# Two graph layers: layer 0's softmax sums by VectorE instead of TensorE, its mask by ScalarE, and the last range check in two parts

## The chip, the core and the metric

The kernel runs on one core of one Trainium2 chip. The metric is the device time of one launch in microseconds (us), the median of several runs. PE is TensorE, PEld its weight loads, DVE is VectorE, ACT ScalarE, POOL GpSimd and SP SyncE.

## What is computed

x is 64 x 256 x 512 and adj 64 x 256 x 256, all float32. adj holds zeros and ones, is symmetric and has ones on its diagonal. Two layers follow one another:

```python
# layer 0
feat_proj = feats @ fc_w.T + fc_b
logits = q + k.T                                  # q, k: one number for each token
masked = logits + (1.0 - adj_mat) * -1e9
masked = where(masked >= 0, masked, 0.01 * masked)
x = softmax(masked, axis=-1) @ feat_proj + feats
# layer 1, 8 heads of 64
scores = Q @ K.T / 8 + (a[:, :, None] + c[:, None, :] + b_g + log(adjacency + 1e-9))
out = softmax(scores, axis=-1) @ V + x
```

## The kernel before

The 64 graphs are worked in 32 groups of two graphs (512 tokens, four blocks of 128). Three groups are in work at once. In `step(d, a, f, n, check)` group `f` goes through layer 0 and the projections of layer 1, group `a` (one before) through layer 1's attention, group `d` (two before) gets its last results divided, completed and stored, and for `n` (one ahead) the inputs are loaded and layer 0's weights made. The order on every engine is written out by hand: strings such as `A("both:0 factor:1:0 pv.sum_10")` name the pieces, and each engine takes its instructions in the order in which the pieces are issued.

**Layer 0's weights.** For group `n`, `adjt` (L538) has DVE turn the adjacency in blocks of 32 into `am` and make `e0 = (am - 1) * 1e9` from it, 128 x 1024. `add_eps` (L548) has ACT add 1e-9 to `am` for layer 1. `weights:0` and `weights:1` (L573) have DVE add q and k to `e0` and apply the leak, and ACT take the exponential. In `e0` the neighbours lie along the partitions and in two tiles `jc`, the tokens in the free dimension. A token's sum is over partitions and both tiles.

**Layer 0's sums.** In the next step, when the group is `f`, `sums` (L586) takes eight matmuls of `e0` with a column of ones in 32 of the array's columns, and ACT copies the result, `sms` (L600). They stand behind `totals_1` of group `d` (L875), which adds up its layer 1 sums with four records of matmuls in 64 columns, and share its PSUM bank. `recip` (L602) turns `sms` by a PE transpose and DVE takes the reciprocal. `mix:0` to `mix:3` (L609) are the products `y` of the unnormalised `e0` with x. `ysum:0` to `ysum:3` (L348) are DVE sums of blocks of y, and `pf` is a product in seven parts, scaled by the reciprocal.

**Attention.** `scores:u` (L789) makes two halves of scores, each in a PSUM pair; there are two such pairs (`psc`, bufs=2). ACT takes the exponential of each half (L815), DVE multiplies it by `am` (`factor`, L821), and `both` (L826) adds the halves.

**The first group** is not mixed with others: `features_first` (L634) writes its order out, with the mask, the weights, the differences of weight blocks on DVE (L333 to L336), the sums, the column constants (L248, L315) and the reciprocal.

**The end.** `finish:gr` (L957) turns, divides and completes the last group's results in two halves `hg` and stores them (`store`, L975; the last ones from SP and ACT). `in_range` (L983) tests that all reciprocals lie between 1e-20 and 1e25; it runs after every fourth group as `check`, and at the end in `check_ranges` (L1026), with a PE transpose and a flag. Every engine loads the flag (L1299) and branches on it (L1301): if a value was out of range, a general version would run.

Of the kernel before, what the change touches and what calls it, by code (L numbers as in the profile page):

```python
# [10 lines left out]
F32 = mybir.dt.float32  # L11
I32 = mybir.dt.int32
AF = mybir.ActivationFunctionType
# [12 lines left out]
def kernel(  # L26
# [97 lines left out]
    nc.gpsimd.memset(eps, 1e-9)  # L124

# [36 lines left out]
    def fast():  # L162
        main = ExitStack()
        with main:
# [349 lines left out]
            class Group:  # L514
# [23 lines left out]
                def adjt(self):  # L538

                    g = self.g  # L540
                    self.am = two.tile([P, TPG, GP, N], F32, tag="am", name=f"am_{g}")
                    self.e0 = one.tile([P, TPG, GP, N], F32, tag="e0", name=f"e0_{g}")
                    flat = "p j g i -> p (j g i)"
                    am, e0 = self.am.rearrange(flat), self.e0.rearrange(flat)
                    nc.vector.transpose(am, self.a.rearrange("p j b c -> p (j b c)"))
                    nc.vector.tensor_scalar(e0, am, 1.0, 1e9, ALU.subtract, ALU.mult)
# [39 lines left out]
                def sums(self):  # L586

                    sm = sm0.pop("bank", None)
                    begun = sm is not None
                    sm = (sm if begun else bank(f"sm0_{self.g}"))[:, 0:P]  # L590
                    for jc in range(TPG):
                        for t in range(T):
                            gr, ic = divmod(t, TPG)
                            nc.tensor.matmul(  # L594
                                sm[ts(t, RS), :], lhsT=ones[:, 0, :], rhs=self.e0[:, jc, gr, ts(ic, P)],
                                start=(jc == 0 and not begun), stop=(jc == TPG - 1),
                                tile_position=(0, t * RS), skip_group_check=True,
                            )
                    self.sms = one.tile([P, P], F32, tag="sms", name=f"sms_{self.g}")
                    nc.scalar.copy(self.sms, sm)  # L600

                def recip(self):  # L602
                    pt = bank(f"rc_{self.g}")[:, 0:P]
                    nc.tensor.transpose(pt, self.sms, ident)
                    nc.vector.reciprocal(
                        recip0[:, self.g, :], pt.rearrange("p (t r) -> p t r", t=T)[:, :, 0]
                    )
# [26 lines left out]
                def features_first(self):  # L634
# [31 lines left out]
                    self.adjt()  # L666
                    product(1)
# [8 lines left out]
                    self.sums()  # L676
# [198 lines left out]
                def totals_1(self):  # L875

                    sm0["bank"] = bank(f"tot_{self.g}_1")
                    self.totals(1, sm0["bank"][:, P : P + NC * N // B])
# [78 lines left out]
                def finish(self, gr):  # L957


                    g, nb = self.g, N // B  # L960
                    self.osb[gr] = two.tile([P, NC * N], F32, tag="osb", name=f"osb_{g}_{gr}")
                    for hg in range(2):
                        o = self.osb[gr][:, ts(hg, 512)]
                        blocks = o.rearrange("p (m c) -> p m c", c=B)
                        nc.vector.transpose(o, self.oTs[gr][:, hg, :])
                        nc.vector.tensor_tensor(
                            blocks, blocks,
                            self.rs[:, ts(hg, 2)].rearrange("p n b -> p (n b)").unsqueeze(2).to_broadcast(
                                [P, 2 * nb, B]
                            ), ALU.mult,  # L970
                        )
                        nc.vector.tensor_tensor(o, o, self.xb[gr][:, ts(hg, 512)], ALU.add)
                    self.store(gr, 2 * (nc.sync, nc.scalar) if gr else 4 * (nc.sync,))
# [9 lines left out]
            def in_range(lo, hi, name):  # L983

                n0, n1 = (hi - lo) * T, (hi - lo) * GP * NC * N // B
                ok = one.tile([P, n0 + n1], F32, tag="junk", name=f"ok_{name}")
                for src, a, b in ((recip0[:, lo:hi].rearrange("p g t -> p (g t)"), 0, n0),
                                  (recip1[:, lo % NR : lo % NR + hi - lo].rearrange(
                                      "p g a h b -> p (g a h b)"), n0, n0 + n1)):
                    nc.vector.tensor_scalar(ok[:, a:b], src, R_LOW, None, ALU.is_ge)  # L990
                    nc.vector.scalar_tensor_tensor(
                        ok[:, a:b], src, R_HIGH, ok[:, a:b], ALU.is_le, ALU.mult
                    )
                okp = const.tile([P, 1], F32, tag=f"okp_{name}", name=f"okp_{name}")
                nc.vector.tensor_reduce(okp, ok, AX.X, ALU.min)
                if "all" in checked:
                    nc.vector.tensor_tensor(okp, okp, checked["all"], ALU.min)
                checked["all"] = okp

            def attention_and_layer_0(D, A, F, X, check):  # L1000
# [3 lines left out]
                F("sums")  # L1004
                A("scores:1 pv.p3 pv.p4 factor:0:0 factor:0:1")
                D("ratios:1")
                A("both:0 factor:1:0 pv.sum_10 factor:1:1 both:1")
# [18 lines left out]
            def check_ranges():  # L1026

                in_range(NG - NR // 2, NG, "last")
                pk = bank("pok")
                nc.tensor.transpose(pk[0:1, 0:P], checked["all"], ident)  # L1030

                def flag_ready():
                    oks = one.tile([1, 2], F32, tag="oks", name="oks")
                    nc.vector.tensor_reduce(oks[:, 0:1], pk[0:1, 0:P], AX.X, ALU.min)
                    nc.vector.tensor_copy(flag, oks[:, 0:1])

                return flag_ready

            checked, sm0 = {}, {}

            def step(d, a, f, n, check):
# [41 lines left out]
                if n is None:  # L1083
                    if a is not None:
                        a.totals(1, bank("tot_last")[:, 0 : NC * N // B])
                    A("ratios:1 divide:1 complete:1 store:1")
                    F("residual:1 turn_residual:1")

                    F("pv.p2 scores:0 pv.p6 pv.sum_00 factor:0:0 factor:0:1 scores:1 both:0 pv.p7")
                    F("factor:1:0 factor:1:1 both:1 scores:2 pv.p5 sums_1:0 scores:3 pv.sum_11")  # L1090
                    F("ratios_t:0 ratios_r:0 factor:2:0 factor:2:1 pv.p3 pv.p4 factor:3:0 pv.sum_10")
                    F("factor:3:1 attend:0 finish:0 sums_of_e:1 attend:1")
                    F("ratios_t:1 ratios_r:1 finish:1")
                    check_ranges()()
                    return
                X("add_eps")
# [6 lines left out]
            with tc.manual_schedule(engines=ENGINES):  # L1103
# [10 lines left out]
                for g in range(NG):  # L1114
                    n = Group(g + 1) if g + 1 < NG else None

                    def check():

                        if d is not None and (d.g % NR == NR - 1 or d.g == NG - NR // 2 - 1):
                            in_range(d.g // NR * NR, d.g + 1, f"{d.g}")  # L1120
# [218 lines left out]
```

## Time and profile before

| | us |
|---|---|
| median of 3 runs (lowest, highest) | 2345.28 (2344.49, 2346.56) |
| the profiled execution | 2344.13 |
| its span in the profile | 2342.3 |
| DVE's mask, L546, 32 times | 22.2 in all, 0.694 each |
| PE's old sums, L594, 512 records | 20.6 in all |
| PE's old transpose before the reciprocal, L604, 32 times | 8.7 in all, 0.272 each |

The profile is of one execution. Times in it are from the start of the span. A PE product of 128x256 in float32 shows as two records of matmul, and lengths of records overlap; what PE spends is read from start to start. A line of the timeline has the start, the length, the engine, the source line, the operation, what is written from what, and how many instructions are put together; in brackets is the idle time of the engine before it and who ended it.

### The profile page before, as it was taken

The numbers are of one execution on the slowest core, as the hardware profiler recorded it, in microseconds if no ns is written. First come the engines' busy times: TensorE is split into PE (matmuls) and PEld (weight loads), VectorE is DVE, ScalarE is ACT, GpSimd is POOL, SyncE is SP. The second block draws the span as 40 slices with busy tenths as digits, with TensorE's granted clock in tenths as the row PEclk, the third lists the DMA queues.
The fourth block names the chain that finished last, engine by engine and source line by source line (L and its number), as shares of the span: only waits on it lengthen the run. The fifth ranks groups of instructions, "written<-read, shape, count | busy, mean of one in ns | idle before, by whom it ended". The sixth has DMA issues, their size and how long they took to land.

```text
span 2342.3 us, 34561 instructions
## 1 busy us (share of the span) xinstructions
PE 2324.0 (99%) x13203; PEld 1907.7 (81%) x13203; DVE 2083.5 (89%) x3026; ACT 980.7 (42%) x1710; POOL 130.4 (6%) x111
## 2 busy tenths in 40 slices
PE   9999999999999999999999999999999999999997
PEld 5888888888888888888888888888888888888885
DVE  6798989889889989999899889998998989999897
ACT  3444344444444344444434444434444344444443
POOL 0000000000000000000000000000000000000000
PEclk9999999999999999999999999999999999999999
DMA  4122332223322233322233232332223332223312
GB/s 131 46 59 73 77 82 59 63 64 86 77 73 55 59 81 77 77 61 59 71 78 81 61 64 61 86 77 72 58 61 77 78 79 62 56 71 81 77 50 38
DMA packets 517267, 163.90 MB, mean 70 GB/s; under 512 B 415188, under 2 KB 478696, under 8 KB 517096
## 3 DMA queue, kind: packets, MB, share of 16 engines
q1 hardware_dynamic: 505512, 156.25, 28.9%
q10 hardware_dynamic: 11584, 5.38, 0.8%
q8 instruction: 107, 1.75, 0.3%
q14 instruction: 64, 0.52, 0.1%
HBM read 95.43 MB, written 66.12 MB: 69 GB/s over the span
## 4 chain that ended last, share of the span: by engine, by line
PE 97%; DVE 2%; DMA 1%; issue 0%; ACTq 0%; ACT 0%; DVEq 0%
PE pv L408 17%; PE pq L408 16%; PE pk L408 16%; PE pf L408 16%; PE sc L801 11%; PE y L626 9%; PE oT L841 9%; PE tot L594 1%; DMA x1T<-xd 1%; PE fp L655 1%; PE tot L868 0%; DMA xd<-xt 0%; DVE t1b L373 0%; DMA fc_nat<-in_L_gnn_fc_w_dram 0%; DVE xt L729 0%
## 5 line engine op out<-in xcount | busy, mean ns | idle before, releaser
L821 DVE TENSOR_TENSOR e<-e,am 128x1024 f32<-128x1024 f32 x254 | 303.3, 1215 | 49.7 <-ACT e L815 49.6
L815 ACT ACTIVATE e<-sc,c 128x1024 f32<-128x1024 f32 x254 | 269.2, 1111 | 42.1 <-PE sc L801 42.1
L801 PE MATMUL sc<-qT,kT 64*128 64x256 f32 x2048 | 255.7, 389 | 0.0
L488 POOL TENSOR_TENSOR pf_s<-pf_s,x 128x512 f32<-128x512 f32 x93 | 128.1, 1378 | 2130.4 <-ACT pf_s L487 2022.5
L841 PE MATMUL oT<-e,v 128*64 128x256 f32 x2032 | 233.4, 382 | 0.0
L801 PEld LDWEIGHTS sc<-qT,kT 64*128 64x128 f32 x2048 | 187.2, 186 | 46.5 <-issue 27.5
L626 PE MATMUL y<-e,x 128*128 128x256 f32 x992 | 222.6, 379 | 0.0
L841 PEld LDWEIGHTS oT<-e,v 128*64 128x64 f32 x2032 | 140.1, 137 | 85.5 <-issue 21.3
L626 PEld LDWEIGHTS y<-e,x 128*128 128x128 f32 x992 | 186.1, 190 | 26.3
L425 ACT ACTIVATE pq_s<-pq,cols 128x256 f32<-128x256 f32 x192 | 80.7, 472 | 255.3 <-PE pq L408 255.3
L487 ACT ACTIVATE pf_s<-pf,recip 128x256 f32<-128x256 f32 x186 | 78.1, 471 | 199.3 <-PE pf L408 198.1
L858 DVE TENSOR_REDUCE part<-est 128x32 f32<-128x1024 f32 x124 | 151.3, 1220 | 4.3
L857 DVE STREAM_TRANSPOSE est<-es 128x1024 f32<-128x1024 f32 x124 | 152.4, 1229 | 0.0
L848 ACT COPY oTs<-oT 128x512 f32<-128x512 f32 x128 | 75.1, 587 | 182.6 <-PE oT L841 161.7
L828 DVE TENSOR_TENSOR es<-e,e 128x1024 f32<-128x1024 f32 x126 | 148.4, 1197 | 1.2
L632 ACT COPY yT<-y 128x512 f32<-128x512 f32 x124 | 72.1, 581 | 152.4 <-PE y L626 152.4
L422 ACT COPY pk_s<-pk 128x512 f32<-128x512 f32 x96 | 56.3, 586 | 186.3 <-PE pk L408 186.3
L422 ACT COPY pv_s<-pv 128x512 f32<-128x512 f32 x96 | 55.6, 579 | 185.4 <-PE pv L408 185.4
L408 PE MATMUL pk<-x1T,wk 128*128 128x256 f32 x512 | 124.2, 385 | 0.0
L408 PE MATMUL pq<-x1T,wq 128*128 128x256 f32 x512 | 121.2, 379 | 0.2 <-DMA x1T<-xd 0.2
L408 PE MATMUL pv<-wv,t1b_c 128*128 128x256 f32 x512 | 121.1, 379 | 0.0
L408 PE MATMUL pv<-wv,t1b 128*128 128x256 f32 x512 | 121.1, 379 | 0.0
(176 smaller groups left out, 4466.9 us busy)
## 6 DMA issues: line engine op xcount, KB each, us to landing
x<-in_x_dram SPq DMA_DIRECT2D x32, 1024.0 KB, 5.2
out_dram<-osb SPq DMA_DIRECT2D x254, 128.0 KB, 3.3
xd<-xt SPq DMA_DIRECT2D x124, 256.0 KB, 2.1
x1T<-xd SPq DMA_DIRECT2D x434, 64.0 KB, 2.0
adj<-in_adj_dram SPq DMA_DIRECT2D x128, 128.0 KB, 3.8
qrow<-q SPq DMA_DIRECT2D x31, 256.0 KB, 4.1
x1T<-xd ACTq DMA_DIRECT2D x62, 64.0 KB, 2.5
fc_nat<-in_L_gnn_fc_w_dram ACTq DMA_DIRECT2D x4, 256.0 KB, 3.9
```

Of the source, the lines that this page charges most:

```text
L408: nc.tensor.matmul(o, lhsT=lk[:, ts(m, P)] if len(lk.shape) == 2 else lk[:, m], rhs=rk, start=(start and m == 0 and k == 0), stop=(m == 1 ...
L422: nc.scalar.copy(dst, src)
L425: nc.scalar.activation(dst[:, m], src[:, m], AF.Identity, bias=self.bias[:, 2 * o + m : 2 * o + m + 1],)
L488: nc.gpsimd.tensor_tensor(s, s, self.out(o, k), ALU.add)
L626: nc.tensor.matmul(y[:, ts(gr, N)], lhsT=self.x[:, gr * TPG + j, ts(c, P)], rhs=self.e0[:, j, gr, :], start=(gr == 0 and j == 0), stop=(gr ...
L801: nc.tensor.matmul(sc[:, par, pr, :], lhsT=self.kT[rows, 2 * hg + pr, ts(t, P)], rhs=self.qT[rows, 2 * hg + pr, ts(gr, N)], start=True, st ...
L815: nc.scalar.activation(e, sc, AF.Exp, bias=self.c[:, t : t + 1], scale=SCALE)
L821: nc.vector.tensor_tensor(ef, ef, self.am[:, jc, u // 2, :].unsqueeze(1).to_broadcast([P, 4, N]), ALU.mult,)
L828: nc.vector.tensor_tensor(self.esum[u], self.e[u, 0], self.e[u, 1], ALU.add)
L841: nc.tensor.matmul(oT[par * HD : (par + 1) * HD, pr, :], lhsT=self.v[:, gr * TPG + jc, ts(h, HD)], rhs=self.e[2 * gr + hg, jc][:, par, pr, :],
L857: nc.vector.transpose(turned, self.esum[u].rearrange("p a b i -> p (a b i)"))
L858: nc.vector.tensor_reduce(self.part[:, hg, :], turned.rearrange("p (m c) -> p m c", c=B), AX.X, ALU.add,)
```

## The change

Layer 0's sums: DVE adds the two tiles of `e0` (`add_tiles`), turns the result in blocks of 32 and sums over 32 (`parts_0`), which leaves four partial sums a token, spread over the four bands of 32 partitions. `recip` adds these with four matmuls of a matrix `every` (which has ones where the places in a band agree), each in 32 columns, and DVE takes the reciprocal from PSUM. The matmuls of `sums`, their copy by ACT and the transpose in `recip` go; `totals_1` has a bank to itself. `add_tiles` stands where `sums` stood, `parts_0` after `ratios:1`, and `factor:1:0` now comes before `both:0`.

The mask: two ACT instructions, just before `add_eps` (in the first group just after `adjt`), in place of one on DVE.

The end: the check of all but the last graph's ratios runs between the halves of `finish:0`, that of the last graph's before `finish:1:0`, the flag is set between `finish:1:0` and `finish:1:1`, and the stores follow as before. For this `finish(gr)` becomes `finish(gr, hg)`, the body of its former loop, with the stores issued apart, and `in_range` takes a list of parts, with the same instructions for each part.

```diff
+    minus = const.tile([P, 1], F32, tag="minus", name="minus")
+    nc.gpsimd.memset(minus, -1.0)
...
-                    am, e0 = self.am.rearrange(flat), self.e0.rearrange(flat)
-                    nc.vector.transpose(am, self.a.rearrange("p j b c -> p (j b c)"))
-                    nc.vector.tensor_scalar(e0, am, 1.0, 1e9, ALU.subtract, ALU.mult)
+                    am = self.am.rearrange(flat)
+                    nc.vector.transpose(am, self.a.rearrange("p j b c -> p (j b c)"))
+
+                def mask(self):
+                    flat = "p j g i -> p (j g i)"
+                    am, e0 = self.am.rearrange(flat), self.e0.rearrange(flat)
+                    nc.scalar.activation(e0, am, AF.Identity, bias=minus)
+                    nc.scalar.mul(e0, e0, 1e9)
...
-                def sums(self):
...
+                def add_tiles(self):
+                    self.es0 = two.tile([P, TOK], F32, tag="xt", name=f"es0_{self.g}")
+                    e0, es0 = self.e0, self.es0.rearrange("p (g i) -> p g i", g=GP)
+                    nc.vector.tensor_tensor(es0, e0[:, 0], e0[:, 1], ALU.add)
+
+                def parts_0(self):
+                    turned = two.tile([P, TOK], F32, tag="xt", name=f"es0t_{self.g}")
+                    self.part0 = one.tile([P, TOK // B], F32, tag="part0", name=f"part0_{self.g}")
+                    nc.vector.transpose(turned, self.es0)
+                    nc.vector.tensor_reduce(
+                        self.part0, turned.rearrange("p (m c) -> p m c", c=B), AX.X, ALU.add
+                    )
 
                 def recip(self):
-                    pt = bank(f"rc_{self.g}")[:, 0:P]
-                    nc.tensor.transpose(pt, self.sms, ident)
-                    nc.vector.reciprocal(
-                        recip0[:, self.g, :], pt.rearrange("p (t r) -> p t r", t=T)[:, :, 0]
-                    )
+                    pt = bank(f"rc_{self.g}")[:, 0:T]
+                    for q in range(P // B):
+                        nc.tensor.matmul(
+                            pt[ts(q, B), :], lhsT=every[:, 0:B],
+                            rhs=self.part0.rearrange("p (t q) -> p q t", q=P // B)[:, q],
+                            start=True, stop=True, tile_position=(0, q * B),
+                        )
+                    nc.vector.reciprocal(recip0[:, self.g, :], pt)
...
                     self.adjt()
+                    self.mask()
...
-                    self.sums()
+                    self.add_tiles()
+                    self.parts_0()
...
                 def totals_1(self):
-                    sm0["bank"] = bank(f"tot_{self.g}_1")
-                    self.totals(1, sm0["bank"][:, P : P + NC * N // B])
+                    self.totals(1, bank(f"tot_{self.g}_1")[:, 0 : NC * N // B])
...
             def attention_and_layer_0(D, A, F, X, check):
...
                 D("totals_1")
-                F("sums")
+                F("add_tiles")
                 A("scores:1 pv.p3 pv.p4 factor:0:0 factor:0:1")
                 D("ratios:1")
-                A("both:0 factor:1:0 pv.sum_10 factor:1:1 both:1")
+                F("parts_0")
+                A("factor:1:0 both:0 pv.sum_10 factor:1:1 both:1")
                 check()
                 F("mix:0 mix:1 ysum:0 recip")
...
+            def check_last(part):
+                if part == 0:
+                    r0, r1 = of_groups(NG - NR // 2, NG)
+                    in_range((r0, r1[:, 0 : r1.shape[1] - NC * N // B]), "last")
+                    return
+                in_range((recip1[:, NR - 1, 1].rearrange("p m b -> p (m b)"),), "graph")
+                pk = bank("pok")
+                nc.tensor.transpose(pk[0:1, 0:P], checked["all"], ident)
+                checked["row"] = pk
+
+            def set_flag():
+                oks = one.tile([1, 2], F32, tag="oks", name="oks")
+                nc.vector.tensor_reduce(oks[:, 0:1], checked["row"][0:1, 0:P], AX.X, ALU.min)
+                nc.vector.tensor_copy(flag, oks[:, 0:1])
...
-                    F("factor:3:1 attend:0 finish:0 sums_of_e:1 attend:1")
-                    F("ratios_t:1 ratios_r:1 finish:1")
-                    check_ranges()()
+                    F("factor:3:1 attend:0 finish:0:0")
+                    check_last(0)
+                    F("finish:0:1 store:0 sums_of_e:1 attend:1 ratios_t:1 ratios_r:1")
+                    check_last(1)
+                    F("finish:1:0")
+                    set_flag()
+                    F("finish:1:1 store_last")
                     return
-                X("add_eps")
+                X("mask add_eps")
                 F("pv.p2 pv.p6")
                 X("weights:0")
```

## The prediction

> **What bounds the kernel now.** I read the page first (busy times, then the chain that ended last), then the groups kept apart by form, then the timeline of one group in mid-run, of the first 45 us and of the end.
>
> ```profile
> PE 2324.0 (99%) x13203; PEld 1907.7 (81%) x13203; DVE 2083.5 (89%) x3026; ACT 980.7 (42%) x1710; POOL 130.4 (6%) x111
> PE 97%; DVE 2%; DMA 1%; issue 0%; ACTq 0%; ACT 0%; DVEq 0%
> ```
>
> TensorE (PE) is the bound: 97% of the chain. VectorE (DVE) is 89% busy but is on the chain only at the two ends. So in the 30 middle groups a change counts by what it does to PE's stream, and DVE work counts only where it doesn't fit into DVE's waits. At both ends DVE time counts in full.
>
> ```profile
> 1155.16 2.00 PE L801 MATMUL sc<-qT,kT 64*128 64x256 f32 x16
> 1156.34 2.12 ACT L815 ACTIVATE e<-sc,c 128x1024 f32<-128x1024 f32 x2
> 1157.09 0.31 PE L868 MATMUL tot<-part,every 128*64 128x32 f32 x4
> 1157.33 0.65 PE L594 MATMUL tot<-e,ones 128*32 128x128 f32 x16
> 1157.49 2.36 DVE L821 TENSOR_TENSOR e<-e,am 128x1024 f32<-128x1024 f32 x2 [0.86 <-ACT e L815]
> 1157.90 2.00 PE L801 MATMUL sc<-qT,kT 64*128 64x256 f32 x16
> 1159.83 1.99 PE L408 MATMUL pv<-v_s,t1b_c 128*128 128x256 f32 x8
> 1163.59 0.69 DVE L436 TENSOR_TENSOR v<-pv,pv_s 128x512 f32<-128x512 f32 x1 [1.26 <-PE pv L408]
> 1166.84 0.27 PE L604 MATMUL rc<-ident,sms 128*128 128x128 f32 x1
> 1166.95 3.62 PE L626 MATMUL y<-e,x 128*128 128x256 f32 x16
> 1167.66 0.69 DVE L348 TENSOR_TENSOR tb<-yT 128x512 f32<-128x512 f32 x1 [0.99 <-ACT yT L632]
> ```
>
> In these timeline lines (start, length, what) the old sums occupy PE from 1157.33 to 1157.90, 0.57 us from start to start, and the old transpose before the reciprocal from 1166.84 to 1166.95, 0.11 us. DVE waits 0.86, 1.26 and 0.99 us in the same stretch.
>
> ```profile
> 2298.26 1.89 PE L408 MATMUL pk<-t1b,wk 128*128 128x256 f32 x8
> 2300.08 0.31 PE L868 MATMUL tot_last<-part,every 128*64 128x32 f32 x4
> 2300.31 1.99 PE L408 MATMUL pv<-wv,t1b_c 128*128 128x256 f32 x8
> 2302.24 2.00 PE L801 MATMUL sc<-qT,kT 64*128 64x256 f32 x16
> ```
>
> This is the price of putting a small block of another tile shape between 128x128 products. The chain has 40 such products in 8.63 us, 0.216 each, so 8 take 1.73. Here the 8 before the block take 1.82 (+0.09), the block 0.23, and the 8 after it 1.93, of which I give half of the +0.20 to the switch in and half to the switch out to the scores: 0.09 + 0.23 + 0.10 = 0.42 us.
>
> **Steady groups, PE.** The sums go: up to 0.57 us. But the second scores then start earlier, and they need the two PSUM pairs that the exponentials of the first scores read. Those are the two in the line at 1156.34: together 2.12, 1.11 each, so the first ends at 1157.45 and the second at 1158.46. Without the sums the scores would come 0.24 after 1157.09 (as at tot_last), at 1157.33, before either has ended. The first half can start at about 1157.50. The second half's weights wait until about 1158.51, and its matmuls follow some 0.1 later, at 1158.6, where they started half of 1.93 after 1157.90, at 1158.87. So 0.24 of 0.57 us is left. ACT can't start those exponentials earlier: it reaches them straight from the copy of pv and layer 0's exponential, which wait for PE's pv block. Ends: 0 and 0.57. I take 0.24. In the first of the 31 mixed groups no totals stand there, the sums fill this very wait, and its weights already wait 0.20 for the exponential, so I count nothing for it.
>
> The reciprocal's new form is four matmuls of 32 columns, 8 records, where one transpose cost 0.11. The block sits between the y products, which are 128x128, so the nearest row is tot_last's 0.42; eight records four abreast are about two rounds, as its four records are two rounds two abreast. Ends: 0.11 (no switch shows) and 0.50. I take 0.44, so +0.33. Steady: 30 x (-0.24) + 31 x 0.33 = -7.2 + 10.2 = +3.0 us.
>
> The Trainium skill, "TensorE: Matmul & The Clock Gate", "Back-to-back issue gap", has small matmuls no closer than about 25 ns whatever their width. Eight would then take 0.20 where two rounds of the tot_last row take about 0.1, and the steady term would be about 3 us larger, an estimate from that page. The sixteen records in 0.57 us of this trace, 36 ns each with streaming included, don't decide it.
>
> **Steady groups, DVE and ACT.** New on DVE: an add of 128x512 (0.69, L436), a turn of 128x512 (0.71, L729) and a sum to 16 (half of L858's 1.22, with its fixed part about 0.66): 2.06 us. Gone: the mask, 0.69 (22.2 us in 32). The add comes when layer 0's second exponential is done (ACT is through at 1156.4), in the 0.86 wait. The turn and the sum delay both:0 and factor:1:0 by about 1.3 us and use up the 1.26 wait before pv.sum_10; 0.99 remain before ysum:0. Nothing on PE waits: its next need of DVE is ysum:1, done at 1172.56 for a product at 1173.86. Where the range check adds some 1.65 us (8 groups), it takes this 0.99 as now. If that cover were gone, about 1.4 us net per group would go to PE, 43 us in all. GpSimd's one more memset and ACT's lost copy of the sums (0.27) lie beside other work.
>
> The mask moves to ACT: two passes of 128x1024, priced by add_eps's group.
>
> ```profile
> L550 ACT ACTIVATE am<-am,eps 128x1024 f32<-128x1024 f32 x32 | 36.8, 1151 | 0.0
> ```
>
> In the middle groups ACT has 3.54 us idle after add_eps, before the copy of pv's sixth product. The two passes, 2.30, fit; behind them are only add_eps and that copy. DVE's first weights wait about 0.3 us for the mask, which the 0.86 wait takes. Steady price: 0.
>
> The new tiles take the two buffers of the sends' xt, whose last readers are 30 us back, and e0 was last read by parts:2, 10 us before the mask: no new wait.
>
> **The start.**
>
> ```profile
> 33.44 0.36 DVE L315 TENSOR_TENSOR cols<-cols,pct 128x2 f32<-128x2 f32 x4 [0.52 <-PE pct L311]
> ```
>
> Here the chain runs over DVE from 33.44 to 42 us, and this line of the timeline shows its only slack: 0.52. Now the turned adjacency is there at 22.5 and the weights start at 23.3. With ACT's two passes they start at 22.5 + 2 x 1.15 + 0.05 = 24.85: 1.55 late. The add, turn and sum stand in front of the column copy: 2.06 more. Less 0.52: +3.1 us, all on the path. Ends: 2.3 and 3.6 (no slack usable).
>
> The Trainium skill, "ScalarE: Activation LUTs", "Rules for kernel authors", advises VectorE, not ScalarE, for adds and multiplies. Its section on the cost of ACT_TABLE_LOAD prices 128x1024 at 1.13 us with a bias column and 1.04 without, an estimate of 2.17 for both; the start would lose 3.0 by the page, 3.1 by the row. The trace agrees that one DVE pass (0.69) is cheaper.
>
> **The end.** These are two lines of the view of L1301, the branch on the flag (length, then first and last start).
>
> ```profile
> L1301 PEldq COMPARE_BRANCH x1: 4716/4716/4716, 2336.5 to 2336.5; - x1
> L1301 SPq EVENT_SEMAPHORE  x8: 17/17/17, 2338.2 to 2339.2; - x8
> ```
>
> Now finish:1 ends on DVE at 2333.1, the last stores are issued at 2333.1, the check follows, and the flag is written at 2335.4. Every engine loads it for about 1 us and branches; PE's branch takes 4.7 us, and SP waits for it 1.1 us and for DVE's 0.7 before the end at 2342.3. SP's semaphore waits show the stores landed at 2338.2 to 2339.2, so the store path alone would end at 2342.3 - 1.8 = 2340.5. After: the first check (1.2 us of small DVE instructions, by the 1.35 of the six of now), the second (0.7) and the flag's reduce and cast (0.45) all stand before the last half result. The flag is set at about 2333.3, two us earlier; the last stores are issued 1.2 + 0.7 + 0.45 = 2.3 later. SP and ACT load the flag behind these stores, DVE behind finish:1:1, about where it did. The store path ends at 2340.5 + 2.3 = 2342.8: +0.5 us, from -0.7 (stores land faster alone) to +1.5. store:0 goes 1.2 later on SP, with nothing queued behind it but the last stores.
>
> **Sum.** +3.0 + 3.1 + 0.5 = +6.6 us. The profiled execution took 2344.13 (2342.3 of span); its sum is 2350.7. It was 1.15 us under the median 2345.28, so against the median I forecast 2352.
>
> **Rivals.**
> (a) The exponentials don't hold the scores back, and the 0.57 us is won whole: 30 x (-0.57) + 10.2 + 3.6 = -3.3, 2342: not slower. For it: PE is 97% of the chain, and ACT has 0.27 us less to do. Against: the two lengths at 1156.34. It decides if the second one ends before about 1158.2.
> (b) The four small matmuls cost no switch: 31 x 0 - 7.2 + 3.6 = -3.6, 2342. For it: totals after attention (64 columns before it too) start without a gap. Against: tot_last. With (a) too: 2345.3 - 17.1 + 3.6 = 2332, faster.
> (c) DVE becomes the bound where the range check falls: 0.9 us more in each of 8 groups, 2359; in every group, 2395. Against: the waits above. It decides if ysum:1 comes over 1.3 us late.
> (d) The end does what it says and the store path isn't late: -2 instead of +0.5, 2349.5, within the forecast's range.
>
> **How the numbers follow.** The forecast has 0.64, its own range 2347 to 2357 from the ends of the start (2.3 to 3.6), the reciprocal (0.3 to 0.5) and the scores (0.1 to 0.35). (a) 0.14, (b) 0.07, both 0.04, (c) 0.11 in both sizes. About 0.2% (4.7 us) is what a measurement can tell from no change. Faster (under 2340.6): both, and a part of (a) and (b) where 0.06 us a group more is won: 0.13. Same: the rest of these and the forecast's low end, 0.21. Slower: 0.66. The range 2341 to 2358 leaves out "both", a little of (a) and (b), and most of (c).
>
> **What would show it.** Right: no L594 left; the second scores some 0.25 us after the totals but with a wait for ACT's exponentials of 0.1 to 0.2 us a group; y products before and after the new block 0.1 us longer; a group's period up by 0.1 from 71.86; DVE at L315 near 36.5; the flag near 2339.4 (2333.3 and the 6.1 before it) and the end set by SP's wait for stores. Wrong: a period of 71.6 or less (a, b), 73 or more with PE waiting for tb or t1b (c), or weights at 23.3 at the start.

## The result and the profile after

The changed kernel takes 2354.66 us (median of 6 runs, 2351.83 to 2355.46), the kernel before 2344.89 beside it (6 runs, 2343.09 to 2346.56): a ratio of 1.0041, 95% interval 1.0028 to 1.0053, 9.8 us slower. The forecast was 2352, slower, with a range of 2341 to 2358. A second set of runs gave 2354.01 against 2344.12, 1.0045 (1.0031 to 1.0058).

The profiled execution took 2354.23 us, its span 2352.5, 10.1 more than the span before. Two lines of the page, busy times and the chain of work that ended last:

```profile
PE 2325.2 (99%) x12915; PEld 1897.0 (81%) x12915; DVE 2127.0 (90%) x3094; ACT 1045.6 (44%) x1742; POOL 123.9 (5%) x112
PE 93%; ACT 3%; DVE 2%; DMA 2%; issue 0%; ACTq 0%; SPq 0%; DVEq 0%
```

PE issues 288 matmul records fewer, and its busy time is not lower but 1.2 us higher. On the chain ACT now has 3% where it had none: something on PE waits for ACT.

The new instructions cost what the rows of before said: by their groups ACT's two passes take 1.152 and 1.057 us, DVE's add, turn and sum 0.682, 0.656 and 0.686.

**Where the 10.1 us lie.** I cut the span at points that both traces have: the first y product (83.54 us before, 91.53 after), the last `tot` (2264.55 and 2272.90; `tot_last` comes later), and the end. The start is 7.98 longer, the 30 groups in between 0.36 and the end 1.76.

**A steady group** in the timeline:

```profile
1163.19 2.00 PE L814 MATMUL sc<-qT,kT 64*128 64x256 f32 x16
...
1165.54 0.73 PEld L814 LDWEIGHTS sc<-qT,kT 64*128 64x128 f32 x8 [0.23 <-ACT e L828]
...
1166.55 0.73 PEld L814 LDWEIGHTS sc<-qT,kT 64*128 64x128 f32 x8 [0.27 <-ACT e L828]
...
1167.61 1.99 PE L410 MATMUL pv<-v_s,t1b_c 128*128 128x256 f32 x8
...
1171.17 3.62 PE L637 MATMUL y<-e,x 128*128 128x256 f32 x16
...
1174.71 0.24 PE L613 MATMUL rc<-part,every 128*32 128x4 f32 x8
1174.89 3.72 PE L637 MATMUL y<-e,x 128*128 128x256 f32 x16
...
1178.45 1.89 PE L410 MATMUL pf<-fcT,yT 128*128 128x256 f32 x8
```

The old sums are gone, but both halves of the second scores now wait for ACT's exponentials. From the first scores to pv it is 4.42 us where it was 4.67: 0.25 of the sums' 0.57 is left. From the first y products to pf it is 7.28 where it was 7.02: the new block costs 0.26. The two cancel; the usual period, from one group's first y product to the next one's, is 71.87 us, 71.86 before. DVE still waits 0.74 before ysum:0, so its cover held.

**The start.** DVE turns the adjacency at 23.82 and starts the reciprocal at 39.80: 15.98 us, where it was 12.69 (21.22 to 33.91). In the timeline of before:

```profile
21.22 1.24 DVE L545 STREAM_TRANSPOSE am<-adj 128x1024 f32<-128x1024 f32 x1
...
33.34 3.60 PE L687 MATMUL x1p<-fp,e 128*128 128x512 f32 x8
...
33.91 0.18 DVE L605 RECIPROCAL recip<-rc 128x4 f32<-128x4 f32 x1
...
42.66 1.89 PE L408 MATMUL pq<-x1T,wq 128*128 128x256 f32 x8
```

And after:

```profile
23.82 1.24 DVE L547 STREAM_TRANSPOSE am<-adj 128x1024 f32<-128x1024 f32 x1
...
39.37 0.24 PE L613 MATMUL rc<-part,every 128*32 128x4 f32 x8 [2.74 <-DVE cols L250]
...
39.54 5.40 PE L700 MATMUL x1p<-fp,e 128*128 128x512 f32 x8
...
39.80 0.18 DVE L618 RECIPROCAL recip<-rc 128x4 f32<-128x4 f32 x1
...
50.65 1.89 PE L410 MATMUL pq<-x1T,wq 128*128 128x256 f32 x8
```

PE waits 2.74 us for DVE, and the eight x1p records behind the wait (the first group's weights times its projected features) take 5.40 us where they took 3.60. The table by stretches gives the reason in its column PEclk, the granted clock (the third number from the end; the columns before it are the busy times of PE, PEld, DVE, ACT and POOL):

```profile
17.50:20.00 2.50, 2.50 (x15) 2.28 (x14) 2.40 (x8) 1.55 (x3) 0.00 (x0) 0.61 1.01 386
...
40.00:45.00 5.00, 5.00 (x11) 2.09 (x10) 3.20 (x5) 0.00 (x0) 0.00 (x0) 0.67 0.00 0
```

Behind the wait PE ran at 0.67 of its clock over 5 us. It also ran at 0.50 to 0.61 from 12.5 to 20 us, ahead of any instruction that the change touches on this path; in the first profile of before it ran at 1.00 in all these stretches. So the 7.98 us are 2.6 of a later start (the turn at 23.82 instead of 21.22), 3.3 of longer DVE work, and 2.1 between the reciprocal and the first product of q, 10.85 instead of 8.75. The turn comes at 21.2 to 22.7 us in the ten profiles on record with the full clock before 20 us, and at 23.0 to 23.8 in the four without it.

**The end**, in the view of L1329, the branch on the flag:

```profile
L1329 SPq EVENT_SEMAPHORE  x8: 17/17/17, 2350.0 to 2350.9; - x8
...
L1329 PEldq COMPARE_BRANCH  x1: 3832/3832/3832, 2342.4 to 2342.4; - x1
```

PE's branch starts at 2342.4 and is over at 2346.3. SP's waits for the stores pass at 2350.0 to 2350.9, 3.7 us later, and end the kernel. Before, they passed at 2338.2 and PE's branch was last, over at 2341.2.

### The profile page after: what moved, and what is told of

Its sections match the earlier page's. It is cut to its first block, busy times and chain, and to the rows that moved or that the text cites. A ratio compares the mean times of both kernels' runs of the same rounds, so it can differ in the third digit from the quotient of the medians.

```text
span 2352.5 us, 34086 instructions
## 1 busy us (share of the span) xinstructions
PE 2325.2 (99%) x12915; PEld 1897.0 (81%) x12915; DVE 2127.0 (90%) x3094; ACT 1045.6 (44%) x1742; POOL 123.9 (5%) x112
## 4 chain that ended last, share of the span: by engine, by line
PE 93%; ACT 3%; DVE 2%; DMA 2%; issue 0%; ACTq 0%; SPq 0%; DVEq 0%
PE pv L410 17%; PE pk L410 16%; PE pq L410 16%; PE pf L410 16%; PE y L637 9%; PE oT L854 9%; PE sc L814 8%; ACT e L828 1%; ACT pv_s L424 1%; ACT e L592 1%; DMA x1T<-xd 1%; DMA xd<-xt 0%; DMA x<-in_x_dram 0%; PE x1p L700 0%; DVE t1b L375 0%
## 5 line engine op out<-in xcount | busy, mean ns | idle before, releaser
L490 POOL TENSOR_TENSOR pf_s<-pf_s,x 128x512 f32<-128x512 f32 x93 | 121.6, 1307 | 2145.2 <-ACT pf_s L489 2075.9
L637 PE MATMUL y<-e,x 128*128 128x256 f32 x992 | 227.5, 382 | 0.0
L410 PE MATMUL pq<-t1b,wq 128*128 128x256 f32 x512 | 121.0, 379 | 0.0
```

The source lines that it names most:

```text
L410: nc.tensor.matmul(o, lhsT=lk[:, ts(m, P)] if len(lk.shape) == 2 else lk[:, m], rhs=rk, start=(start and m == 0 and k == 0), stop=(m == 1 ...
L490: nc.gpsimd.tensor_tensor(s, s, self.out(o, k), ALU.add)
L637: nc.tensor.matmul(y[:, ts(gr, N)], lhsT=self.x[:, gr * TPG + j, ts(c, P)], rhs=self.e0[:, j, gr, :], start=(gr == 0 and j == 0), stop=(gr ...
```

## The experiments

Differences are against the kernel before, timed on the same chip beside each run; its median was 2344.1 to 2345.0 on all of them, so medians from different chips are also compared with each other.

**before_again** is the unchanged kernel, for a second profile.

> The kernel before once more, for a second look at the first 20 us, where the changed kernel's PE was already 3.7 us late before any changed instruction. Theory 1 (the early delay belongs to the change or its neighbourhood): PE's clock is full from 12.5 to 20 us, the first product fp starts near 16.2, y of the first mixed group near 83.5, span near 2342. Theory 2 (it is chance of an execution): some executions of this kernel show it too; this profile may have the clock near 0.55 there, fp near 19.9 and a span some 3.5 us longer. Time: no change, ratio 1.000.

2345.03, ratio 1.0002 (0.9993 to 1.0011). The first y product comes at 84.61 us (83.54 in the first profile), with the same two stretches, 12.69 and 8.75. Three experiments then split the change into its parts.

**mask_only**: the kernel before with the mask by ScalarE.

```diff
-                    nc.vector.tensor_scalar(e0, am, 1.0, 1e9, ALU.subtract, ALU.mult)
...
+                    nc.scalar.activation(e0, am, AF.Identity, bias=minus)
+                    nc.scalar.mul(e0, e0, 1e9)
...
-                X("add_eps")
+                X("mask add_eps")
```

> Only the mask by ACT. Theory 1: start +1.0 (1.55 less 0.52 of slack), middle groups unchanged at 71.86 with DVE's weights waiting 0.3 to 0.4 us for ACT in each, end 0: +1 us. Theory 2 (ACT's two passes delay ACT's copies in every group): 72.0 or more a group, +4 us or more.

2346.72, 1.0010 (1.0001 to 1.0019), so +2.0 us. In its profile the reciprocal comes 14.23 us after the turn of the adjacency, 1.54 later than before: the 1.55 of the forecast, of which DVE's 0.52 of slack was to save a part and saved none. PE waits 0.93 us for ACT's copy of fp, where it didn't wait before, so the delay came along ACT and PE too, and DVE still has 0.48 of its slack. PE's clock stays at 1.00, the reciprocal-to-q stretch is 8.75, and the usual period is 71.86: in the steady groups the two passes on ACT cost nothing.

**sums_only**: the kernel before with `add_tiles`, `parts_0` and the new `recip`.

```diff
-                    self.sums()
+                    self.add_tiles()
+                    self.parts_0()
...
-                F("sums")
+                F("add_tiles")
...
-                A("both:0 factor:1:0 pv.sum_10 factor:1:1 both:1")
+                F("parts_0")
+                A("factor:1:0 both:0 pv.sum_10 factor:1:1 both:1")
```

> Only layer 0's sums by DVE, with the new reciprocal; mask and end as before. Theory 1: start +1.5 (DVE's 2.06 less 0.52 of slack; PE stands for less than 2 us, so its clock stays full), middle groups 71.87 (the exponentials take back 0.25 to 0.3 of the 0.57, the four small matmuls cost 0.26 more than the transpose), end 0: +2 us in all. If DVE were the cause in the middle: 72.3 or more a group, +13 us. If the sums were a gain: 71.6 or less, -6 us.

2349.34, 1.0021 (1.0012 to 1.0030), +4.65 us, where +2 was expected. In its profile the DVE chain is 1.96 longer (14.65), the usual period is 71.87, and PE waits 1.67 before the reciprocal's matmuls, with the clock at 1.00 behind it and 9.16 to q. That is 2.4 us at the start and 0.3 in the steady groups; the other 2 us of the 4.65 this profile doesn't show.

**end_only**: the kernel before with the end of the changed one.

```diff
-                    F("factor:3:1 attend:0 finish:0 sums_of_e:1 attend:1")
-                    F("ratios_t:1 ratios_r:1 finish:1")
-                    check_ranges()()
+                    F("factor:3:1 attend:0 finish:0:0")
+                    check_last(0)
+                    F("finish:0:1 store:0 sums_of_e:1 attend:1 ratios_t:1 ratios_r:1")
+                    check_last(1)
+                    F("finish:1:0")
+                    set_flag()
+                    F("finish:1:1 store_last")
```

> Only the split check and the flag between the halves; layer 0 as before. Theory 1: nothing up to tot_last; from there to the end 44.1 us where it was 42.2, +1.9 us, with the last stores issued 2.4 us later and SP waiting for them. Theory 2 (the end gains what the flag gains): 40.2 us, -2 us.

2347.55, 1.0011 (1.0002 to 1.0020), +2.9 us; from the last totals to the end 79.05 us instead of 77.53 in before_again. Its PE clock was 0.50 to 0.62 from 12.5 to 20 us, although nothing there differs from before: the low clock before 20 us is not of the change's making. The parts add up: 2.0 + 4.65 + 2.9 = 9.5.

**first_old**: the changed kernel, with the first group's mask and sums as before.

```diff
-                    self.mask()
+                    self.mask_dve()
...
-                    self.add_tiles()
-                    self.parts_0()
+                    self.sums_old()
...
-                    self.recip()
+                    self.recip_old()
```

> The changed kernel, but in the first group alone the mask is DVE's and the sums, their copy and the transpose before the reciprocal are PE's and ACT's, as before; the other 31 groups and the end stay changed. Theory 1 (the start costs what the first group's new work costs: 3.3 us more from the turned adjacency to the reciprocal and 2.1 us of a lower PE clock behind PE's wait for it): the reciprocal comes 12.7 us after the turn of the adjacency instead of 16.0, the first product of q 8.75 us after the reciprocal instead of 10.85, and the time falls by 5.4 us from 2354.7 to about 2349. Theory 2 (most of the start's loss is chance, the low clock before 20 us, which no edit touches): the time stays within 1.5 us of 2354.7. Theory 3 (the predicted 3.1 us and nothing behind it): about 2351.5.

2348.34, 1.0013 (1.0004 to 1.0022), 6.3 us under the changed kernel. The two stretches are 12.69 and 8.75 again. So the first group alone, one of 32, makes about two thirds of the loss. Theory 1 stands, theory 3 (3.1 alone) falls short.

**warm**: the changed kernel with products of no use where PE waits.

```diff
                     add_constants()
+                    idle = bank("idle")
+                    for _ in range(20):
+                        nc.tensor.matmul(idle[:, 0:P], lhsT=ident, rhs=ident, start=True, stop=True)
                     self.recip()
```

> The changed kernel with 20 products of 128x128 of the identity with itself (results not read) on PE in the first group, just before the reciprocal's small matmuls, where PE waits 2.74 us for DVE. Theory 1 (PE's clock falls because PE stands idle there): the granted clock in 40 to 45 us is 1.00 instead of 0.67, the eight x1p records take 3.6 us instead of 5.4, the first product of q comes 8.75 us after the reciprocal instead of 10.85, and the time falls by about 2 us from 2354.7. Theory 2 (the clock falls there for another reason, as before 20 us): x1p still takes 5.4 and the time is that of the changed kernel, within 1 us. A third outcome: the products run past DVE's column copy and PE is late by up to 0.5 us.

2352.02, 1.0032 (1.0021 to 1.0043), 2.6 us faster than the changed kernel with more work on PE. The two intervals overlap, and the profile decides. Its table by stretches and its timeline:

```profile
40.00:45.00 5.00, 5.00 (x19) 2.58 (x18) 4.53 (x8) 0.82 (x3) 0.00 (x0) 1.00 0.00 0
```

```profile
33.77 4.63 PE L695 MATMUL idle<-ident 128*128 128x128 f32 x40
...
38.50 3.70 PE L703 MATMUL x1p<-fp,e 128*128 128x512 f32 x8
```

The clock is 1.00, and x1p takes 3.70. The third outcome came as well: the products filled PE until 38.4, and the reciprocal came 16.45 us after the turn, 0.5 later. The lower clock is the price of PE standing idle. The executions without a profile agree: the mean clock of each whole run is 0.995 to 0.997 in the 11 of the changed kernel, and 0.997 or 0.998 in warm's 7 and first_old's 11.

How long it waits depends on how late PE itself is, as the profiles with the new sums in the first group show (sums_only has the old mask; the third column is read below):

| profile | PE's wait | most of it in one window | clock at 0.50 | x1p, eight records | reciprocal to q |
|---|---|---|---|---|---|
| sums_only | 1.67 | 1.67 | none | 3.70 | 9.16 |
| the changed kernel | 2.74 | 2.74 | 3.4 | 5.40 | 10.85 |
| after_again | 3.25 | 1.87 | none | 3.70 | 9.16 |
| p3_between | 3.77 | 2.11 | 6.8 | 6.14 | 11.64 |
| rc_move | 3.75 | 2.42 | 6.8 | 6.31 | 11.80 |
| late_flag | 3.75 | 2.98 | 6.8 | 6.58 | 12.08 |

In the first three PE had lost time to the low clock before 20 us, and so came later to the wait. With the full clock before 20 us it waits 3.75, and the stretch behind is 2.9 to 3.3 us longer than 8.75. Of that 0.41 isn't the clock, as the 9.16 at full clock show: 0.17 is the new block on PE, the rest the reciprocal, which follows its matmuls sooner. So the clock cost 1.7 us in the changed kernel and 2.5 to 2.9 in the last three. The two low clocks take each other's place in part: with this first group the first y product comes at 89.2 to 91.5 us in five profiles (mean 90.6), and at 83.5 to 85.0 (mean 84.4) in the five that have the old first group and the full clock. That is 6.2 us, as first_old's 6.3.

What decides whether the clock falls? In shorter stretches the 0.67 of the changed kernel's table is a full half:

```profile
37.50:40.00 2.50, 0.63 (x9) 0.48 (x10) 2.26 (x11) 0.00 (x0) 0.00 (x0) 0.99 0.01 3
40.00:42.50 2.50, 2.50 (x4) 1.01 (x3) 1.25 (x2) 0.00 (x0) 0.00 (x0) 0.50 0.00 0
42.50:45.00 2.50, 2.50 (x8) 1.08 (x7) 1.95 (x3) 0.00 (x0) 0.00 (x0) 0.83 0.00 0
```

Read in slices of 0.5 us from 10 to 47 us, the clock of every profile is 1.00 or 0.50 but for the slices in which it changes, and each low stretch, before 20 us too, lasts 3.4 or 6.8 us. In the changed kernel it is low from 12.6 to 19.5 and from 39.9 to 43.4 us, and the 20.5 us between these are six times 3.41. So the clock changes on a grid of 3.41 us, which lies elsewhere in each run. The third column is the longest part of the wait that falls into one window of this grid, counted on in steps of 3.41 from an edge that the trace shows: with 2.11 us or more the clock fell at the end of that window, with 1.87 or less it didn't. Where the next window still held 0.8 to 1.7 us of the wait, the clock stayed low for a second one. The Trainium skill, "TensorE: Matmul & The Clock Gate", "What's actually happening", says that the clock falls to half after an idle window of about 3.4 us, and that the windows run free of the kernel. The traces agree on the windows, but here one that was idle for 2.1 of its 3.4 us was enough. So the 2.74 lost the clock and the 3.25, which an edge cut in two, didn't.

**rc_move**: the changed kernel with the reciprocal's small matmuls behind the second scores, where the tile shape changes anyway. For this `recip` is parted into its matmuls, `add_bands`, and DVE's reciprocal, `divide_0`.

```diff
-                F("add_tiles")
-                A("scores:1 pv.p3 pv.p4 factor:0:0 factor:0:1")
+                F("add_tiles parts_0")
+                A("scores:1")
+                F("add_bands")
+                A("pv.p3 pv.p4 factor:0:0 factor:0:1")
                 D("ratios:1")
-                F("parts_0")
+                F("divide_0")
...
-                F("mix:0 mix:1 ysum:0 recip")
+                F("mix:0 mix:1 ysum:0")
```

> The changed kernel with parts_0 straight behind add_tiles on DVE and the reciprocal's four small matmuls between the second scores and pv's third part, where the tile shape changes anyway; DVE's reciprocal stands where parts_0 ended before. The first group stays as it is. Theory 1 (of the block's 0.37 us some 0.09 to 0.10 on each side is the change of shape): between the y products nothing stands any more, -0.37, and between scores and pv the block adds 0.18 to 0.28, so that the period falls by 0.1 to 0.2 us and the time by 3 to 6 us from 2354.7. Theory 2 (the 0.37 is the block itself, wherever it stands): the period stays at 71.87. Theory 3 (PE then waits for DVE's parts, which come at 1.4 us later than the add): the period grows, with a wait for DVE before the small matmuls.

2348.31, 1.0016 (1.0007 to 1.0025), 6.35 us under the changed kernel. The usual period is 71.68. Timeline:

```profile
1162.34 2.14 PE L820 MATMUL sc<-qT,kT 64*128 64x256 f32 x16
1164.40 0.25 PE L617 MATMUL rc<-part,every 128*32 128x4 f32 x8
1164.58 1.99 PE L410 MATMUL pv<-v_s,t1b_c 128*128 128x256 f32 x8
1168.14 7.07 PE L643 MATMUL y<-e,x 128*128 128x256 f32 x32
1175.04 3.19 PE L410 MATMUL pf<-fcT,yT 128*128 128x256 f32 x14
```

The y products now take 6.90 from start to start where they took 7.28 with the block between them, so the block cost 0.38 there. Here it costs its own 0.17 to 0.18: scores to pv is 2.24 where it was 2.07. The other 0.20 is the change of shape on its two sides. Theory 1 stands, theory 2 falls.

**p3_between**: the changed kernel with pv's third part before the second scores.

```diff
-                A("scores:1 pv.p3 pv.p4 factor:0:0 factor:0:1")
+                A("pv.p3 scores:1 pv.p4 factor:0:0 factor:0:1")
```

> The changed kernel with pv's third part (eight 128x128 products, 1.9 us) issued between the totals and the second scores instead of behind the second scores. Theory 1 (the exponentials of the first scores hold the second scores in PSUM, so that 0.3 us of the old sums' 0.57 is lost in every group): the waits of the second scores' weights for ACT (0.23 and 0.27 us) are gone, one more change of tile shape costs 0.1, a group's period falls by 0.2 us from 71.87, and the time by about 6 us from 2354.7 to 2349. Theory 2 (the second scores are held by something else, or the wait comes back at pv's third part, whose inputs are late): the period stays within 0.05 of 71.87 and the time within 1.5 us. Against both: the second exponentials come 1.7 us later, and if DVE's factors then come late for attention's products, the period grows.

2349.90, 1.0023 (1.0014 to 1.0032), 4.8 us under the changed kernel. Timeline:

```profile
1160.17 2.00 PE L814 MATMUL sc<-qT,kT 64*128 64x256 f32 x16
...
1164.26 1.60 PEld L814 LDWEIGHTS sc<-qT,kT 64*128 64x128 f32 x16 [0.33 <-issue]
...
1166.19 1.99 PE L410 MATMUL pv<-wv,t1b 128*128 128x256 f32 x8
```

No wait for ACT is left, and the second scores take 1.93 instead of 2.07. From the first scores to pv's fourth part it is 6.02, 0.23 less than 6.25, and 0.10 of that goes to one more change of shape: pv's fourth part, which now follows scores, takes 1.83 instead of 1.73. The period is 71.75: -0.12, not the -0.2 that I expected. So the exponentials did hold the scores.

**late_flag**: the changed kernel with the flag behind the last stores.

```diff
-                    check_last(1)
-                    F("finish:1:0")
-                    set_flag()
-                    F("finish:1:1 store_last")
+                    F("finish:1:0 finish:1:1 store_last")
+                    check_last(1)
+                    set_flag()
```

**after_again** is the changed kernel, for a second profile.

> The changed kernel with the last part of the range check and the flag moved behind the last half result and its stores; the first part of the check stays between the halves of the first graph's results. The last stores are then issued about 1.2 us earlier against the last totals than in the changed kernel, and the flag about 2 us later. Theory 1 (the end is the later of two paths, and the stores, issued 2.4 us later, have passed the branch's): the branch is last again, the time from the last totals to the end is that of before, 77.6 us instead of 79.5, and the time falls by about 2 us. Theory 2 (the stores land 1 us later after their issue because the branch's instructions are fetched at the same time, and this is what costs): stores land 5.1 us after issue again, and the time falls by 1 us only if the branch does not become last. Rival: the split of the check itself, or the first part of it between the halves, is the cost: the time stays within 0.5 us of the changed kernel's.

> The changed kernel as it is, for a second profile and more times. Theory 1 (the first 20 us at half clock in the first profile of the changed kernel were chance): the profile shows a clock of 1.00 from 12.5 to 20 us, DVE turns the adjacency near 22.2 instead of 23.8, and the median lies one to two us under 2354.7, near 2353, with 8 us over the kernel before: 3.3 for the first group's longer DVE chain, 2 to 3 for PE's clock behind its wait, 0.2 for the steady groups and 1.9 for the end. Theory 2 (the change brings the low clock before 20 us about): the profile shows 0.5 to 0.6 there again and the median stays at 2354.7.

after_again: 2354.01, as given above. Its clock was 0.63 to 0.68 from 12.5 to 17.5 us, so theory 1 didn't get the profile that it foretold. That clock falls in 4 of 14 profiles, among them end_only's; in p3_between, rc_move, warm and late_flag, which share the new first group, it doesn't. What sets it stays open.

late_flag: 2354.41, 1.0042 (1.0028 to 1.0056). The time doesn't tell it from the changed kernel, with intervals of 3 us either way; the profile does. From the last totals to the end it takes 78.4 us (79.56 and 79.65 in the profiles of the changed kernel, 77.80 and 77.53 in those of before), and the view of its branch, at L1328, has PE last again, at 2352.3, where its branch of 4.87 us ends:

```profile
L1328 SPq EVENT_SEMAPHORE  x8: 17/17/17, 2349.7 to 2351.3; - x8
...
L1328 PEldq EVENT_SEMAPHORE  x1: 51/51/51, 2352.3 to 2352.3; - x1
```

So there are two paths, as theory 1 has it, but only 1.2 of the 2 us come back: the first part of the check still stands before both. Theory 2's observation held too. With the flag behind the stores SP's first wait passes 5.1 us after their issue, and 4.3 to 5.2 in the six profiles of the old end; with the flag before them it is 6.1 to 6.3 in five of seven profiles, and 4.7 in two. Whether the code that the branch fetches delays the stores was not separated.

**both_old_ends**: both moves, with first group and end as before. Against the changed kernel, beside the diff of first_old and the end of before:

```diff
-                F("add_tiles")
-                A("scores:1 pv.p3 pv.p4 factor:0:0 factor:0:1")
+                F("add_tiles parts_0")
+                A("pv.p3 scores:1")
+                F("add_bands")
+                A("pv.p4 factor:0:0 factor:0:1")
                 D("ratios:1")
-                F("parts_0")
+                F("divide_0")
...
-                F("mix:0 mix:1 ysum:0 recip")
+                F("mix:0 mix:1 ysum:0")
```

> The changed kernel in its steady groups alone, with both moves: pv's third part between the totals and the second scores, and the reciprocal's small matmuls straight behind the second scores, parts_0 behind add_tiles; first group and end as before the change. Measured alone, the moves took a group's period from 71.87 to 71.75 and to 71.68. If they add up: 71.56, so -0.30 x 30 = -9 us against the kernel before, near 2336. If the waits they remove are the same, or DVE's parts come late for the small matmuls: 71.68 or more and 2340 or more. If DVE, which has 1.4 us more to do in each group and less slack in this order, holds PE: over 2345.

2335.84 (2335.27 to 2336.88), ratio 0.9965 (0.9951 to 0.9978): 8.3 us faster than before, and faster than both kernels. The usual period is 71.55, so the moves add up (-0.12 and -0.19 from 71.87 make 71.56). Timeline:

```profile
1151.34 2.00 PE L846 MATMUL sc<-qT,kT 64*128 64x256 f32 x16
...
1157.36 0.24 PE L644 MATMUL rc<-part,every 128*32 128x4 f32 x8
1157.53 1.99 PE L410 MATMUL pv<-wv,t1b 128*128 128x256 f32 x8
```

**small_together**: the same, with the totals behind the reciprocal's matmuls, and on DVE their ratios behind layer 0's reciprocal.

```diff
                 A("pv.sum_11 scores:0")
-                D("totals_1")
                 F("add_tiles parts_0")
                 A("pv.p3 scores:1")
                 F("add_bands")
+                D("totals_1")
                 A("pv.p4 factor:0:0 factor:0:1")
-                D("ratios:1")
                 F("divide_0")
+                D("ratios:1")
```

> both_old_ends with the totals of layer 1 moved from between the first scores and pv's third part to just behind the reciprocal's small matmuls, so that the two small blocks stand together between the second scores and pv's fourth part. Theory 1 (the price of a small block is mostly the change between a large block's tile shape and another one, paid once on each side): two small blocks together share their sides, and the period falls by about 0.1 us from 71.55, the time by about 3 us from 2335.8. Theory 2 (a change of shape costs the same between small blocks): the number of changes is the same, and so is the period, within 0.03. Rival: the ratios' reciprocal on DVE, which waits for the totals, now holds DVE, and the period grows.

2337.39, 0.9970 (0.9957 to 0.9982), period 71.55: theory 2. Timeline:

```profile
1152.57 2.00 PE L846 MATMUL sc<-qT,kT 64*128 64x256 f32 x16
1154.50 1.99 PE L410 MATMUL pv<-v_s,t1b_c 128*128 128x256 f32 x8
1156.42 2.00 PE L846 MATMUL sc<-qT,kT 64*128 64x256 f32 x16
...
1158.53 0.31 PE L913 MATMUL tot<-part,every 128*64 128x32 f32 x4
1158.77 1.99 PE L410 MATMUL pv<-wv,t1b 128*128 128x256 f32 x8
```

From the first scores to pv's fourth part it is 6.20, and 6.19 in both_old_ends: as many changes of shape, the same time. The Trainium skill, "TensorEngine Tiling (Array Packing)", "Key Properties", says that a change of tiling mode drains TensorE, and gives no price. Here pv's eight products take 1.92 with scores on both sides; the rows of before gave 1.82 for eight such products with a change on one side, and 1.73 with none.

## Why the prediction was right, and where its steps weren't

The total was right: slower, 2352 forecast, 2354.66 measured. Its terms were not all right, and that the sum came within 3 us is partly luck: 2.6 us too much in the steady groups stand against 2.3 too little at the start and 1.3 too little at the end.

- **Second scores: right.** -0.24 a group forecast, -0.25 measured, with the waits of 0.23 and 0.27 for ACT's exponentials where I placed them. p3_between shows the cause by removing it. Rival (a) falls.
- **Reciprocal: right in kind, too large.** +0.33 forecast, +0.26 measured: the eight records took 0.18 instead of the 0.23 taken from the totals. That is 22 ns each, while the forecast's other estimate, with 25 a record, would have made the block larger still. rc_move splits it into 0.18 and 0.20. Rival (b) falls: the switch costs. Over 31 groups the difference made the steady term +3.0 where the period shows 30 x 0.01 = 0.3.
- **DVE and ACT in steady groups: right.** The cover held, and rival (c) didn't come.
- **Start: the DVE chain right, its consequence missed.** +3.1 forecast, +3.3 measured. The step that failed is "+3.1 us, all on the path" as the whole price: PE, idle while DVE is late, loses its clock, which cost 1.7 us more in this profile and 2.5 to 2.9 in three others; 0.4 more behind the reciprocal comes at full clock too. Nothing in the trace of before showed a wait of that length at this place, but the wait itself followed from my own sum, and I didn't follow it to PE.
- **End: path right, price too small.** Stores issued 2.3 us later by the forecast, 2.4 measured; the end set by SP's waits, as forecast. +0.5 was the term; +1.8 measured. The assumption that the stores land as soon after their issue as before failed: 6.1 us instead of 5.1. Rival (d) falls.

By the changed kernel's first profile the terms are 0.4 + 5.4 + 1.8 = 7.6 us, and 2.6 of the late turn. Those 2.6 are not the change's, but without them PE would have waited longer and lost more behind the wait: with the 6.2 us of the five profiles instead, the sum is 0.4 + 6.2 + 1.8 = 8.4, inside the measured 6.6 to 12.4 (0.28% to 0.53% of 2344.89).

## What to carry to other kernels

Work taken off the bound engine is worth only what the next wait leaves. Here half of it was lost to PSUM that ACT still read, and the rest to a small block with a change of tile shape on each side; with one block moved into the wait, and the small one to where the shape changes anyway, a group took 0.31 us less than before the change. Price a change apart for the first group and the end: there the engines that are covered elsewhere are the path, and 1 group of 32 cost more here than the other 31 together. When an engine is made late, ask what its consumer does meanwhile: a TensorE that stood idle for a little over 2 us of one window came back at half speed here.

## What the runs showed of the hardware

- PE's granted clock is 1.00 or 0.50 and changes on a grid of 3.41 us that lies elsewhere in each run. It fell in four profiles where a wait filled 2.11 to 2.98 us of one window, and not in two where it filled 1.67 and 1.87; eight x1p records then took 5.4 to 6.6 us instead of 3.6. Products of no use in the wait kept it at 1.00, in a kernel 2.6 us faster.
- The same clock is at 0.50 for 3.4 or 6.8 us before 20 us in 4 of 14 profiles, with the kernel's code there unchanged. PE was idle for about 0.5 us at most of the window before, so what sets it there is not the wait above, and stays open.
- A change of tile shape costs about 0.10 us on the side of a block of 128x128 products (eight of them take 1.73, 1.82 and 1.92 us with none, one and two changes beside them). Two small blocks side by side cost as much as apart (6.20 and 6.19).
- A branch on PE took 3.4 to 4.9 us; the last stores, issued behind its start, mostly took 1 us longer to be seen by SP.
